# A graph attention layer on one core: 250 blocks, and destination terms with the one-hots as moving side

## The chip, the cores and the metric

The kernel runs on one core of one Trainium2 chip. It is written against the engines directly: TensorE (PE, with its weight loads as PEld), VectorE (DVE), ScalarE (ACT), GpSimd (POOL) and SyncE (SP, which issues most transfers). Each engine runs its instructions in the order in which the program gives them, and engines wait for one another by semaphores. The metric is the device time of one execution, in microseconds; lower is better.

## The reference

The input is a graph of 30000 nodes with 256 features and 510000 directed edges, sorted by destination, each of one of 8 types. One layer is computed: attention over incoming edges, then a feed-forward part with experts.

```python
feat_all = jnp.einsum('ni,rhid->rnhd', inputs, conv_weights)   # 8 types, 4 heads of 64
feat_src_e = feat_all[edge_type, edge_src]
feat_dst_e = feat_all[edge_type, edge_dst]
el = jnp.sum(feat_src_e * attn_l[edge_type], axis=-1)
er = jnp.sum(feat_dst_e * attn_r[edge_type], axis=-1)
e = jax.nn.leaky_relu(el + er, negative_slope=0.2)
m = jax.ops.segment_max(e, edge_dst, num_segments=N_NODES)
ex = jnp.exp(e - m[edge_dst])
alpha = ex / segment_sum(ex, edge_dst)[edge_dst]
h = segment_sum(alpha[..., None] * feat_src_e, edge_dst)       # + h_bias
...
x = x + gnn(layernorm(x))
x = x + ffn(layernorm(x))      # a shared MLP, and the best 2 of 4 small experts by a softmax gate
```

The score of an edge has a source term `el` and a destination term `er`, one number for each head. The change is about how `er` gets from the nodes to the edges.

## The kernel before

**Node stage.** Tiles of 128 nodes are normalised, transposed on TensorE (two transposes a tile) and multiplied by the weights of all types and heads (L304). For each node and type, a row of `feat` in DRAM gets 4 heads of 64 features with `el` as a 65th column. `er` of each node goes to `erp_d`, as three bf16 pieces whose sum is the f32 value: 4 heads x 3 pieces x 8 types = 96 columns. Between the matrix products a generator, `aside`, is asked for one small step once a tile (twice a tile after the edge records are done). Its steps prepare the edges: `edge_records` writes a record of each edge and finds the bounds of the blocks; `places` makes, for batches of 12 blocks, the lists `rk_d` (per place: index of the source row, destination, marks, penalties, and `th`, which is 1 at the edge's type and 0 at the 7 others) and `dk_d` (the destinations as 16-bit integers). `first_rows` gathers the first row of each block.

**Blocks.** The edges are cut into blocks that begin at the first destination at or after a multiple of S = 2016, with room for CAP = 2048 edges and 128 destinations. That is 252 blocks and one last block of another form. A block's edges are laid out as 128 partitions x 16 places. If a block has too many edges or nodes, or the edges are not sorted, a flag (`bad`) makes a general second pass run after this one.

**Edge loop.** It is unrolled over the blocks `t`, and each turn has six parts, c = 0 to 5, in which pieces of several blocks are put one after another by hand. The rest of the program is this order: there is no other planner. In a turn,

- `load(t+2)` asks SyncE for the block's lists, its `dr` (the destinations, copied to all partitions), `erp` (the 96 columns of the block's up to 128 nodes) and the residual; `gather(t+1)` has GpSimd fetch 15 rows of `feat` per partition (L962), SyncE the first one from `stage`;
- `dest_select` (L1009, VectorE) compares `dr` with the node numbers: a one-hot of node by edge, 128 x 2064 in bf16, in c = 4 for block t+2;
- `dest_expand` (L1026, TensorE) multiplies each of 16 columns of places (one-hot as the stationary side, 128 x 128) with `erp` (96 moving columns), four in each of four pieces; `dest_pick` (L1037, L1039, VectorE) multiplies a piece by `th` and sums over types and pieces of bf16, which gives `er` of the edges. The first piece of block t+2 is done in c = 4 and 5, the others of block t+1 in c = 0 to 3;
- `scores` (L1066 on, in c = 1) adds `er` and `el` and starts the running maxima along the destinations; `turn_ends` (TensorE, L993 and L994, c = 2), `across` (VectorE, L1084, c = 3) and `turn_back` (TensorE, L1091 and L1092, c = 4) carry them over the partitions; `softmax` (L1098 on) and `exps` come in c = 5;
- `onehot` (ScalarE, L1049 and L1050) builds the one-hot of edge by node in f32; `weigh` (VectorE, L1115) multiplies the gathered rows by the weights; `sums` (TensorE, L1122) multiplies the two, for block t-1, one sixth in each part; `finish` (L1144 to L1147) divides;
- one step of `Experts` (the feed-forward part for a group of four finished blocks: L754 to L877) is taken in each part. Its four results go out by SyncE (`put`).

An f32 matmul shows as two records on TensorE. The buffers that matter are: `dr`, `erp` and `ohT` two each, `pe` (the result of the expansion in PSUM) two, the gathered rows four blocks in a ring.

Of the kernel before, what the change touches and what calls it, by code (L numbers as in the profile page):

```python
# [10 lines left out]
F32 = mybir.dt.float32  # L11
BF16 = mybir.dt.bfloat16
# [23 lines left out]

U = 16
CAP = U * P
S = 2016
# [9 lines left out]
WR = WT + U * R // 2  # L49
# [7 lines left out]
def kernel(  # L57
# [40 lines left out]
    erp_d = dram.tile([N + P, H, 3, R], BF16, name="erp_d")  # L98
# [4 lines left out]
    rk_d = dram.tile([NBLK, P, WR], I32, name="rk_d")  # L103
    dk_d = dram.tile([NBLK * CAP + 16], I16, name="dk_d")
    stage = dram.tile([NBLK * P, H * HW], F32, name="stage")
# [3 lines left out]
    lo_d = dram.tile([KT, P], F32, name="lo_d")  # L109
    n_d = dram.tile([KT, P], F32, name="n_d")  # L110
    uns_d = dram.tile([EP], F32, name="uns_d")
    mnmx = dram.tile([2, NGRP], F32, name="mnmx")
# [21 lines left out]
    def layernorm(pool, xg, n, name, m=P):  # L134
# [10 lines left out]
        for t in range(n):  # L145
# [28 lines left out]
                   allow_small_or_imprecise_dtypes=True)  # L174
    icol = wf.tile([P, P], F32, name="icol")
# [45 lines left out]
    with ExitStack() as cx:  # L221
# [102 lines left out]
        def dest_pieces(q, n):  # L324

            er = quad.pop((q, "er"))
            del quad[q]
            erp = xp.tile([P, T, H, 3, R], BF16, name="erp")
            erv = er.rearrange("p j (r h) -> p j h r", h=H)[:, :n]
            for k in range(3):  # L330
                nc.vector.tensor_copy(erp[:, :n, :, k, :], erv)
                if k < 2:
                    nc.vector.tensor_sub(erv, erv, erp[:, :n, :, k, :])
            per_rows(q, lambda r, n: erp_d[r:r + n].rearrange("n h k r -> n (h k r)"),
                     lambda p, j: erp.rearrange("p j h k r -> p j (h k r)")[p, j], True)
# [9 lines left out]
        def edge_records(cl):  # L345
# [55 lines left out]
            nc.sync.dma_start(erp_d[N:N + P].rearrange("n h k r -> n (h k r)"),  # L401
                              zx.bitcast(BF16)[:, :R * 3 * H])
            yield

# [3 lines left out]
            dw = gp.tile([P, KT, WN + 1], I32, name="dw")  # L408
            nc.gpsimd.memset(dw, -1)
            jj = gp.tile([P, WN], F32, name="jj")  # L410
            nc.gpsimd.iota(jj, pattern=[[1, WN]], base=0, channel_multiplier=0,
                           allow_small_or_imprecise_dtypes=True)
            first = gp.tile([P, KT], F32, name="first")
            irow = gp.tile([P, 1], F32, name="irow")
# [6 lines left out]
            nc.sync.dma_start(dw[0:1, 0, 1:], dst[0:WN].rearrange("(o c) -> o c", o=1))  # L421
            for k in range(KT):
                a = 1 if k == 0 else 0
                n = min(P, NBLK + 1 - k * P)
                nc.sync.dma_start(dw[a:n, k, :],
                                  bass.AP(tensor=dst.tensor, offset=dst.offset + (k * P + a) * S - 1,
                                          ap=[[S, n - a], [1, WN + 1]]))
            before_last = gp.tile([1, 1], I32, name="before_last")
            nc.sync.dma_start(before_last, dst[E - UL * P - 1:E - UL * P].rearrange("(o c) -> o c", o=1))
            yield  # L430
            lof = gp.tile([P, 2, KT], F32, name="lof")
            miss = gp.tile([P, KT, WN], F32, name="miss")
            nc.vector.tensor_tensor(miss, dw[:, :, 1:], dw[:, :, :WN], op=ALU.is_equal)
            yield
            for i, v in enumerate((jj[:, None, :].to_broadcast([P, KT, WN]), dw[:, :, 1:])):
                cand = gp.tile([P, KT, WN], F32, name="cand")
                nc.vector.scalar_tensor_tensor(cand, miss, FAR, v, op0=ALU.mult, op1=ALU.add)
                nc.vector.tensor_reduce(lof[:, i, :], cand, AX.X, ALU.min)
                yield
            nc.vector.tensor_add(lof[:, 0, :], lof[:, 0, :], first)  # L440
            nc.vector.tensor_scalar_min(lof[:, 0, :], lof[:, 0, :], float(E))
            nc.vector.tensor_scalar(lof[:, 1, :], lof[:, 1, :], 0.0, float(N), op0=ALU.max, op1=ALU.min)
            yield
            lor = gp.tile([1, KT * P], F32, name="lor")
            nr = gp.tile([1, KT * P], F32, name="nr")
            with nc.allow_non_contiguous_dma(reason="first edges and nodes of blocks, once"):
                for i, (t_d, row) in enumerate(((lo_d, lor), (n_d, nr))):
                    nc.sync.dma_start(t_d.rearrange("k p -> p k"), lof[:, i, :])
                    yield
                    if i:  # L450
                        nc.sync.dma_start(t_d[0:1, 0:1], zx[0:1, 0:1])
                        yield
                    nc.sync.dma_start(row, t_d.rearrange("(o k) p -> o (k p)", o=1))
                    yield
# [7 lines left out]
            unm = gp.tile([EP, 1], F32, name="unm")  # L462
# [5 lines left out]
            unr = gp.tile([1, EP], F32, name="unr")  # L468
# [3 lines left out]
            two = gp.tile([1, 5], F32, name="two")  # L472
            gap = gp.tile([1, NBLK], F32, name="gap")
# [9 lines left out]
            nc.vector.tensor_reduce(bad, two, AX.X, ALU.max)  # L483

# [5 lines left out]
        def places(cl):  # L490
# [35 lines left out]
            for k, (b0, n) in enumerate(batches):  # L526
# [40 lines left out]
                d16 = kp.tile([P, GB, U], I16, name="d16k")[:, :n]  # L567
                nc.gpsimd.tensor_copy(d16, rc[:, :, :U, 1])
# [13 lines left out]
                th = o[:, :, WT:].bitcast(BF16).rearrange("p b (u r) -> p b u r", r=R)  # L582
                for b in range(0, n, GB // 2):
                    m = min(n - b, GB // 2)
                    nc.vector.tensor_tensor(th[:, b:b + m], rc[:, b:b + m, :U, 2:3].to_broadcast([P, m, U, R]),
                                            it8[:, None, :U].to_broadcast([P, m, U, R]), op=ALU.is_equal)
                    yield

                def done(o=o, d16=d16, b0=b0, n=n):
                    nc.sync.dma_start(rk_d[b0:b0 + n].rearrange("b p w -> p b w"), o)  # L590
                    nc.sync.dma_start(dk_d[b0 * CAP:(b0 + n) * CAP].rearrange("(b p u) -> p b u", p=P, u=U), d16)
# [290 lines left out]
    with ExitStack() as cx:  # L882
# [4 lines left out]
        pe_p = cx.enter_context(tc.tile_pool(name="pe", bufs=2, space=PSUM))  # L887
# [34 lines left out]
        def load(t):  # L922
# [3 lines left out]
            if s.own:  # L926
# [12 lines left out]
                s.a12 = rf[:, W1:W1 + 2 * (U + 2)].rearrange("p (i w) -> p i w", i=2)[:, :, :U]  # L939
                s.th = rk[:, WT:].bitcast(BF16).rearrange("p (u r) -> p u r", r=R)  # L940
# [11 lines left out]
            s.erp = lp.tile([P, H, 3, R], BF16, name="erp")  # L952
# [52 lines left out]
        def dest_select(t):  # L1005
# [4 lines left out]
                                    rowid[:, t:t + 1], None, op0=ALU.is_equal)  # L1010
            s.ov = ohT[:, :n * P].rearrange("n (p u) -> n u p", u=n)
            if not s.own:
                s.th = wk.tile([P, UL, R], BF16, name="th", bufs=1)
# [6 lines left out]
        def dest_expand(t, c):  # L1020

            s = blk[t]
            u0, u1 = s.dc[c], s.dc[c + 1]
            pe = pe_p.tile([P, 5, H * 3, R], F32, name="pe")
            for u in range(u0, u1):
                nc.tensor.matmul(pe[:, u - u0].rearrange("p f r -> p (f r)"), s.ov[:, u, :],  # L1026
                                 s.erp.rearrange("n h k r -> n (h k r)"), start=True, stop=True)
            s.pe = pe

        def dest_pick(t, c):  # L1030

            s = blk[t]
            if c == 0:
# [420 lines left out]
```

## Time and profile before

The median of 11 runs is 8525.87 us (8505.01 to 8543.13). The profiled execution took 8503.86 us.

| | |
|---|---|
| span of the profiled execution | 8502.1 us, 97367 instructions |
| its own time | 8503.86 us |
| PE busy | 6501.1 us, 76% |
| PEld busy | 4163.5 us, 49% |
| DVE busy | 5293.6 us, 62% |
| ACT busy | 3414.1 us, 40% |
| POOL busy | 4085.6 us, 48% |
| mean granted TensorE clock | 0.875 |
| mean DMA rate | 143 GB/s |

Busy time is the time in which an engine runs instructions; several run at once. The node stage fills some 1700 us, the edge loop the rest. Line numbers (L1026) are those of the kernel before. In a group's row stand the line, engine, operation, what is written and read with shapes, the count, then busy us and mean ns of one, and after the bar the idle time of the engine just before these, with what ended it. "Remote" stands for a semaphore whose update the profile puts down to no instruction.

### The profile page before, as it was taken

How to read it: one execution, taken by the hardware profiler on the slowest of the kernel's cores; microseconds unless marked ns; L12 is line 12 of the kernel's file. 1: busy time of each engine (PE TensorE's matmuls, PEld its weight loads, DVE VectorE, ACT ScalarE, POOL GpSimd, SP SyncE). 2: the span in 40 equal slices, each digit the busy share in tenths (PEclk: the TensorE clock that was granted, in tenths of full speed). 3: DMA queues.
4: the chain of work that ended last, by engine and by line, in shares of the span. 5: the costliest groups of instructions: out<-in, count | busy, mean ns of one | idle time of the engine just before them, and what ended most of it. 6: DMA issues, size and time to landing. Idle time of an engine off the chain costs nothing. (4 is left out here: it accounts for less than half of the span.)

```text
span 8502.1 us, 97367 instructions
## 1 busy us (share of the span) xinstructions
PE 6501.1 (76%) x25770; PEld 4163.5 (49%) x25771; DVE 5293.6 (62%) x13699; ACT 3414.1 (40%) x8758; POOL 4085.6 (48%) x4424
## 2 busy tenths in 40 slices
PE   9999999937776777777777777777767777776767
PEld 5555555525444444444444444444444444444444
DVE  5557774446666666666666666666666666666665
ACT  2222222224444444444444444444444444444444
POOL 1111115665555555555555555555555555555552
PEclk9999999968888888888888888888888888888888
DMA  6657779954444444444344344343343434433441
GB/s 230 227 184 241 225 241 319 327 178 117 116 117 116 117 116 115 117 117 118 116 117 117 115 116 117 115 116 115 114 116 116 115 116 116 121 113 114 121 116 54
DMA packets 764587, 1214.72 MB, mean 143 GB/s; under 512 B 242499, under 2 KB 602918, under 8 KB 733814
## 3 DMA queue, kind: packets, MB, share of 16 engines
q1 hardware_dynamic: 568581, 668.72, 24.0%
q0 software_dynamic: 194400, 539.40, 22.7%
q8 instruction: 209, 3.42, 0.2%
q14 instruction: 357, 2.92, 0.1%
q10 hardware_dynamic: 1040, 0.26, 0.0%
HBM read 821.54 MB, written 386.43 MB: 142 GB/s over the span
## 5 line engine op out<-in xcount | busy, mean ns | idle before, releaser
L962 POOL DMA_INDIRECT ft<-feat,rk x3798 | 3607.0, 950 | 3035.3 <-PE po L1122 1428.9
L1122 PE MATMUL po<-ft,oh 128*128 128x260 f32 x8100 | 2401.9, 437 | 387.6 <-DVE ho L1147 114.2
L1122 PEld LDWEIGHTS po<-ft,oh 128*128 128x128 f32 x8100 | 1639.9, 216 | 746.9 <-issue 413.6
L304 PE MATMUL ps<-w,xT 128*128 128x448 f32 (+1 forms) x4700 | 1707.4, 518 | 1.8 <-DMA w<-_L_gnn_conv_weights_dram 1.8
L1049 ACT ACTIVATE oh<-icol,rk 128x128 f32<-128x128 f32 x4032 | 1327.7, 389 | 57.1 <-remote 32.1
L1115 DVE TENSOR_TENSOR ft<-ft,p 128x768 f32<-128x768 f32 x1518 | 1292.3, 852 | 69.3 <-ACT ft L1108 49.2
L304 PEld LDWEIGHTS ps<-w,xT 128*128 128x128 f32 x4700 | 875.3, 190 | 688.7 <-issue 602.5
L1026 PE MATMUL pe<-erp,ohT 128*128 128x96 bf16 x4050 | 451.0, 239 | 594.4 <-DVE ohT L1009 320.8
L1037 DVE TENSOR_TENSOR ere<-pe,rk 128x384 f32<-128x384 f32 x1008 | 553.5, 549 | 506.6 <-remote 385.1
L1026 PEld LDWEIGHTS <-ohT 128*128 128x128 bf16 x4050 | 377.8, 158 | 983.8 <-issue 592.2
L306 ACT COPY fo<-ps 128x448 f32<-128x448 f32 (+1 forms) x711 | 377.9, 533 | 1060.0 <-PE ps L304 863.6
L1050 ACT ACTIVATE oh<-oh 128x384 f32<-128x384 f32 x1518 | 740.3, 488 | 55.7 <-remote 5.7
L1039 DVE TENSOR_REDUCE e<-ere 128x16 f32<-128x384 f32 (+1 forms) x1012 | 561.4, 555 | 34.7
L1107 ACT ACTIVATE p<-e 128x64 f32<-128x64 f32 (+1 forms) x253 | 70.1, 277 | 1233.4 <-DVE e L1061 1042.5
L818 PE MATMUL ph<-xT,v 128*128 128x512 f32 (+2 forms) x1024 | 495.1, 607 | 0.9 <-ACT a L819 0.5
L764 ACT COPY xT<-ph 128x512 f32<-128x512 f32 (+1 forms) x128 | 73.6, 575 | 1025.5 <-remote 871.3
L1084 DVE TENSOR_TENSOR_SCAN car<-through,t 8x128 f32<-8x128 f32 x252 | 101.5, 403 | 603.7 <-remote 485.7
L1091 PE MATMUL t<-ident,car 8*128 8x4 f32 x506 | 105.9, 277 | 429.7 <-issue 369.0
L871 PE MATMUL pf<-w,h 128*128 128x256 f32 x506 | 205.7, 495 | 269.4 <-ACT wT L864 213.4
L306 DVE COPY fo<-ps 128x448 f32<-128x448 f32 (+1 forms) x464 | 242.4, 528 | 202.2 <-PE ps L304 170.6
L818 PE MATMUL ph<-xT,w 128*128 128x512 f32 (+1 forms) x512 | 307.5, 731 | 60.8 <-ACT xT L764 34.4
L1091 PEld LDWEIGHTS t<-ident,car 8*128 8x128 f32 x506 | 83.6, 206 | 521.0 <-issue 443.7
(219 smaller groups left out, 7362.7 us busy)
## 6 DMA issues: line engine op xcount, KB each, us to landing
feat<-fo SPq DMA_DIRECT2D x234, 1040.0 KB
dr<-dk_d SPq DMA_DIRECT2D x252, 516.0 KB
ft<-feat,rk POOLq DMA_INDIRECT x3798
stage<-fr SPq DMA_DIRECT2D x84, 390.0 KB
ft<-stage SPq DMA_DIRECT2D x252, 130.0 KB
xt<-xb_d SPq DMA_DIRECT2D x253, 128.0 KB
out_dram<-og SPq DMA_DIRECT2D x253, 128.0 KB
xb_d<-xb SPq DMA_DIRECT2D x58, 512.0 KB
```

Source lines behind the costliest of these rows:

```text
L304: nc.tensor.matmul(ps, t["xT"][:, k, :], w[:, k, c0:c1], start=k == 0, stop=k == 1)
L306: eng(t["fo"][:, h0:h1, :HD], ps[:, :n].rearrange("p (a d) -> p a d", d=HD))
L818: nc.tensor.matmul(ps[:, :self.w], lhs, rhs, start=i == 0, stop=i == len(pairs) - 1)
L871: nc.tensor.matmul(pf[:M], self.h2[:, tok], w3, start=True, stop=False)
L962: nc.gpsimd.indirect_dma_start(out=s.ft[:, u].rearrange("p h d -> p (h d)"), out_offset=None, in_=feat[:, :], in_offset=bass.IndirectOffse ...
L1026: nc.tensor.matmul(pe[:, u - u0].rearrange("p f r -> p (f r)"), s.ov[:, u, :], s.erp.rearrange("n h k r -> n (h k r)"), start=True, stop=True)
L1037: nc.vector.tensor_mul(ere, s.pe[:, :u1 - u0], s.th[:, u0:u1, None, :].to_broadcast([P, u1 - u0, H * 3, R]))
L1039: nc.vector.tensor_reduce(s.e[:, :, u0:u1].rearrange("p h u -> p u h"), ere.rearrange("p u (h k) r -> p u h (k r)", h=H), AX.X, ALU.add)
L1049: nc.scalar.activation(s.oh[:, u, :], icol, AF.Abs, bias=s.nd[:, u:u + 1])
L1050: nc.scalar.activation(s.oh[:, u0:u1], s.oh[:, u0:u1], AF.Relu, bias=1.0, scale=-1.0)
L1115: nc.vector.tensor_mul(fc, fc, pc[:, :, None].to_broadcast([P, (u1 - u0) * H, HD]))
L1122: nc.tensor.matmul(s.po.rearrange("n h d -> n (h d)"), s.oh[:, u, :], s.ft[:, u].rearrange("p h d -> p (h d)"), start=u == 0, stop=u == s. ...
```

## The change

The constant S becomes 2032, so that there are 250 blocks and the last one. A block may now begin at the destination boundary before or after its multiple of S; four candidate lists (edge and node, early and late) are made, and a scan picks for each block the one that keeps it within CAP edges and 128 nodes.

The destination terms change sides. The block's `erp` piece (128 nodes x 32 columns: 4 heads x 8 types) is now the stationary side, and the one-hot of node by edge is the moving side, 512 columns at a time. The four quarters of the block's 2048 places go to the four 32-partition parts of one PSUM bank, and the three bf16 pieces add up there: 12 matmuls, all in c = 0. In `rel_d` each place has its type; it is loaded to the 32 partitions of each quarter by four transfers a block. One VectorE operation (c = 2) compares it with the partition's type and multiplies by the PSUM result. Four f32 matmuls with a 128 x 16 selector (`dest_turn`, c = 3) turn the result back to edges by heads, where `scores` reads it from PSUM. `dest_select` moves from c = 4 to c = 5, behind the softmax. `pe` gets one buffer, `ee` the other.

In the node stage, `places` no longer makes `th`; the lists get shorter by 64 words of 178. The place numbers and types are transposed on TensorE (four transposes a batch) and copied by ScalarE to 16-bit rows, which are stored in four transfers a batch instead of one. The last block keeps the old form.

```diff
-S = 2016
+S = 2032
...
-WR = WT + U * R // 2
+WR = WT
...
+    sel = wf.tile([P, 4 * H], F32, name="sel")
...
+    rid = wf.tile([P, 1], F32, name="rid")
...
+            nc.vector.tensor_tensor_scan(late[:, 1:NBLK + 1], may[:, 1], may[:, 0], 1.0, ALU.add, ALU.max)
...
-                th = o[:, :, WT:].bitcast(BF16).rearrange("p b (u r) -> p b u r", r=R)
-                for b in range(0, n, GB // 2):
-                    m = min(n - b, GB // 2)
-                    nc.vector.tensor_tensor(th[:, b:b + m], rc[:, b:b + m, :U, 2:3].to_broadcast([P, m, U, R]),
-                                            it8[:, None, :U].to_broadcast([P, m, U, R]), op=ALU.is_equal)
-                    yield
-
-                def done(o=o, d16=d16, b0=b0, n=n):
+                yield
+                GH2 = GB // 2
+                ps = pf.tile([P, 512], F32, name="ps").rearrange("q (i f p) -> q i f p", i=2, p=P)
+                rt = kp.tile([GH2 * U, 2, 2, P], I16, name="rt")
+                parts = [(f, b, min(n - b, GH2)) for f, b in enumerate(range(0, n, GH2))]
+                for i in range(2):
+                    for f, b, m in parts:
+                        nc.tensor.transpose(ps[:m * U, i, f], dr2[:, i, b:b + m].rearrange("p b u -> p (b u)"), ident)
+                for f, b, m in parts:
+                    nc.scalar.copy(rt[:m * U, :, f], ps[:m * U, :, f])
+                yield
+
+                def done(o=o, rt=rt, parts=parts, b0=b0, n=n):
                     nc.sync.dma_start(rk_d[b0:b0 + n].rearrange("b p w -> p b w"), o)
-                    nc.sync.dma_start(dk_d[b0 * CAP:(b0 + n) * CAP].rearrange("(b p u) -> p b u", p=P, u=U), d16)
+                    for i, d in enumerate((dk_d, rel_d)):
+                        for f, b, m in parts:
+                            nc.sync.dma_start(d[(b0 + b) * CAP:(b0 + b + m) * CAP].rearrange("(q p) -> q p", p=P),
+                                              rt[:m * U, i, f])
...
-        pe_p = cx.enter_context(tc.tile_pool(name="pe", bufs=2, space=PSUM))
+        pe_p = cx.enter_context(tc.tile_pool(name="pe", bufs=1, space=PSUM))
+        ee_p = cx.enter_context(tc.tile_pool(name="ee", bufs=1, space=PSUM))
...
+                s.rel = lp.tile([P, 4 * P], I16, name="rel")
+                for c in range(4):
+                    e0 = t * CAP + c * 4 * P
+                    nc.sync.dma_start(s.rel[32 * c:32 * c + 32], rel_d[e0:e0 + 4 * P].partition_broadcast(32))
...
         def dest_expand(t, c):
 
-            s = blk[t]
+
+            s = blk[t]
+            if s.own:
+                if c == 0:
+                    s.pe = pe_p.tile([P, 4 * P], F32, name="pe", tag="pe")
+                    for k in range(3):
+                        for q in range(4):
+                            nc.tensor.matmul(s.pe[32 * q:32 * q + 32], s.erp[:, k].rearrange("n h r -> n (h r)"),
+                                             s.ohT[:, q * 4 * P:(q + 1) * 4 * P], start=k == 0, stop=k == 2)
+                return
...
         def dest_pick(t, c):
 
             s = blk[t]
+            if s.own:
+                if c == 0:
+                    s.pick = wk.tile([P, 4 * P], F32, name="pick")
+                    nc.vector.scalar_tensor_tensor(s.pick, s.rel, rid, s.pe, op0=ALU.is_equal, op1=ALU.mult)
+                return
...
+        def dest_turn(t):
+
+            s = blk[t]
+            if not s.own:
+                return
+            s.ee = ee_p.tile([P, 4, 4 * H], F32, name="ee")
+            for j in range(4):
+                nc.tensor.matmul(s.ee[:, j], s.pick[:, j * P:(j + 1) * P], sel, start=True, stop=True)
...
-            nc.vector.tensor_add(s.e, s.e, s.ft[:, :, :, HD].rearrange("p u h -> p h u"))
+            if s.own:
+                s.e = wk.tile([P, H * UL], F32, name="e", bufs=3)[:, :H * U].rearrange("p (h u) -> p h u", h=H)
+                nc.vector.tensor_add(s.e.rearrange("p h (c j) -> p h c j", c=4),
+                                     s.ee.rearrange("p j (c h) -> p h c j", c=4),
+                                     s.ft[:, :, :, HD].rearrange("p (c j) h -> p h c j", c=4))
...
-                        at(dest_pick, t + 2, 0)
-                    if c == 4:
                         at(dest_select, t + 2)
...
-                    if 0 < c < 4:
-                        at(dest_pick, t + 1, c)
+                    if 0 < c < 5 and t + 1 == NBLK:
+                        at(dest_pick, t + 1, c - 1)
...
+                    if c == 2 and t + 1 < NBLK:
+                        at(dest_pick, t + 1, 0)
...
-                    if c == 4:
-                        at(dest_expand, t + 2, 0)
-                    if c < 3:
-                        at(dest_expand, t + 1, c + 1)
+                    if c < 4:
+                        at(dest_expand, t + 1, c)
+                    if c == 3:
+                        at(dest_turn, t + 1)
```

## The prediction

> **What bounds the kernel now.** I began with the busy time by stretch, because a mean over the span mixes two programs. Columns: start:end, length, then busy us (and instructions) of PE, PEld, DVE, ACT and POOL, granted clock, DMA share, GB/s.
>
> ```profile
> 0.00:1600.00 1600.00, 1593.49 (x4794) 865.74 (x4796) 956.44 (x2621) 415.81 (x889) 387.48 (x535) 1.00 0.73 244
> 1900.00:8420.00 6520.00, 4669.83 (x20128) 3151.93 (x20128) 4184.23 (x10664) 2899.48 (x7622) 3506.46 (x3692) 0.85 0.40 116
> 5176.00:5200.00 24.00, 6.86 (x29) 5.09 (x29) 6.66 (x15) 7.69 (x20) 15.25 (x17) 0.70 0.43 124
> 5200.00:5283.00 83.00, 70.50 (x306) 47.84 (x305) 61.92 (x161) 42.32 (x113) 44.05 (x47) 0.90 0.40 115
> ```
>
> The node stage (first row) is all TensorE. In the edge loop (second row) no engine is full: TensorE 72%, VectorE 64%, DMA 40%. The last two rows cut one group of four blocks in two: 24 us in which every engine that computes is mostly idle, and 83 us in which TensorE is 85% busy and VectorE 75%. So most blocks are nearly TensorE-bound, and one place in four blocks is a stall.
>
> Next, the groups of the loop (2200 to 8300 us) for what the change touches.
>
> ```profile
> L962 POOL DMA_INDIRECT ft<-feat,rk x3471 | 3296.6, 950 | 2804.4 <-PE po L1122 1342.1 <-issue 737.6 <-remote 309.7
> L1039 DVE TENSOR_REDUCE e<-ere 128x16 f32<-128x384 f32 x927 | 514.1, 555 | 31.8
> L1037 DVE TENSOR_TENSOR ere<-pe,rk 128x384 f32<-128x384 f32 x927 | 508.9, 549 | 428.9 <-remote 333.3 <-PE po L1122 54.0 <-PE ph L818 19.3
> L1026 PE MATMUL pe<-erp,ohT 128*128 128x96 bf16 x3708 | 412.8, 238 | 513.6 <-DVE ohT L1009 302.1 <-issue 148.8 <-remote 62.7
> L1009 DVE TENSOR_SCALAR ohT<-dr,rowid 128x2064 bf16<-128x2064 int16 x232 | 296.7, 1279 | 0.0
> L858 DVE TENSOR_TENSOR a<-a,ph 128x512 f32<-128x512 f32 x115 | 78.5, 682 | 192.0 <-remote 158.0 <-PE po L1122 27.1 <-PE ph L855 6.4
> ```
>
> 3471 gathers at 15 a block are 231.4 blocks in 6100 us: 26.4 us a block, 105.4 a group. By the shares above a block holds 18.9 us of TensorE and 16.9 of VectorE. GpSimd's gathers need 15 x 1.25 us = 18.8 us, so it isn't the bound.
>
> The stall, in VectorE's timeline (start, duration, what, and idle time before it):
>
> ```profile
> 5188.76 0.41 DVE L1084 TENSOR_TENSOR_SCAN car<-through,t 8x128 f32<-8x128 f32 x1 [11.51 <-remote]
> 5195.87 0.56 DVE L1037 TENSOR_TENSOR ere<-pe,rk 128x384 f32<-128x384 f32 x1 [5.59 <-remote]
> 5196.94 1.28 DVE L1009 TENSOR_SCALAR ohT<-dr,rowid 128x2064 bf16<-128x2064 int16 x1
> 5198.73 0.28 DVE L1098 TENSOR_TENSOR c<-t,rk 128x128 f32<-128x128 f32 x1
> ```
>
> The two waits are for TensorE's semaphore, which moves at 5188.74 and 5195.85, while the records of the matmuls waited for end at 5175.6 and 5175.9. I cannot say what holds these signals. Some 16 us a group go here (24 less the 8 that 6.86 us of TensorE would take at 85%).
>
> **The change, part by part.**
>
> *Two blocks fewer.* 253 blocks become 251: -2 x 26.4 = -53 us. From the reference's destinations I worked out the new bounds: no block over 2048 edges or 128 nodes, so the second pass stays off.
>
> *VectorE.* Out, per block: four products and four sums, 4 x (0.549 + 0.555) = 4.4 us. In: one operation on 128x512 from PSUM, 0.68 us by L858, the nearest row. Net -3.7 us of 16.9. The score addition reads PSUM with the same 64 columns. How much reaches the end? At least nothing, if TensorE alone sets clean blocks. At most 3.4 us, TensorE's idle 15% of a clean block of (105.4 - 16) / 4 = 22.4 us. TensorE's waits on VectorE (one-hots 302, denominators and outputs 251, scan rows 131 us in the loop) are 3.0 us a block, and VectorE's load falls by 22%: 0.7 us. Moving the one-hot build (1.28 us) from part 4, where the expansion and the sums queued behind it, to part 5 behind the softmax adds 0.2. In part 0 the sums already wait for the denominators, so the expansion moved there fills idle time. I take -0.9.
>
> *TensorE, expansion.* Before: four bf16 matmuls and the step to the next line take 0.29 us (5029.00 to 5029.29 below), 1.2 us a block.
>
> ```profile
> 5027.68 0.38 PE L994 MATMUL t<-turned,fb 128*8 128x128 f32 x2
> 5027.99 1.08 PE L843 MATMUL ph<-a,v 128*64 128x512 f32 x4
> 5029.00 0.45 PE L1026 MATMUL pe<-erp,ohT 128*128 128x96 bf16 x4
> 5029.29 0.89 PE L1122 MATMUL po<-ft,oh 128*128 128x260 f32 x3
> ```
>
> After: twelve matmuls of 32 stationary and 512 moving columns, to four quarters of the output partitions. L843 is the row that tells most: two matmuls of 64 columns to two halves start 7 ns apart, and the pair takes 1.01 us where one f32 matmul of full width takes 2 x 0.43 (L818's spacing). So parts side by side cost about what one does. A bf16 matmul of 512 columns is not in the trace: at most 0.43 us (an f32 record of that width), at least half, 0.21; L1026's 63 ns for 96 columns scale to 0.33. I take 0.27, so three rounds of 0.27 and 0.19 for changing the column mode twice (312 ns from L1122 to an 8-column matmul where 219 is its own step) are 1.0 us; bounds 0.8 to 1.5, all overlapped, and 2.7 to 5.3 if nothing overlaps. Four quarters at once have no row.
> The Trainium skill, "TensorE: Matmul & The Clock Gate", Part 3, measured three column tiles at 2.38 times the speed of one, short of three; with that page's 216 ns for one such matmul, four at the same efficiency (3.17) would make the twelve take 12 x 0.216 / 3.17 = 0.8 us, an estimate, and by it the sum would be 0.2 us a block lower, some 30 us at the end. This case's halves (1.01 us against 0.86) agree that parts side by side cost a little more than one, and no run here shows four yet.
>
> *TensorE, turning back.* Four f32 matmuls with 128x128 stationary and 16 moving columns, eight records. The gate matmuls are that shape:
>
> ```profile
> 5204.65 1.84 PE L770 MATMUL pg<-gw,xT 128*128 128x4 f32 x16
> ```
>
> Eight take 0.92 us. TensorE thus gains 1.0 + 0.92 - 1.2 = +0.75 us, and about +0.85 with the half clock that the loop's 0.85 contains. Following the waits back from 8300 to 2200 us, TensorE's own work is some 43% of that path, 61% of its busy time: +0.5 us a block reaches the end. The turn sits in part 3, ahead of the sums there, and waits for the pick of part 2: what queues behind are three sums, whose input VectorE finishes just before the pick, so 0 to 0.7 us; I take 0, as TensorE has two transposed rows, a layer and two sums to do first.
>
> *The stall.* After the late signal VectorE runs L1037, L1039, L1009 and one product before the softmax (L1098), 2.9 us in which others wait. Pick and one-hot are gone from there: up to 2.4 us a group. I take 1.5 x 62 groups = -93 us; bounds below, under the rivals.
>
> *Loads.* SyncE issues four more transfers a block (0.35 to 0.7 us each by its other issues, so about 2 us of 26) and 128 KB more, with 32 KB less of indices. Behind them in its queue are the one-hot source, factors, residual and first rows; the one-hot source of that group was issued at 5166.0 and used at 5196.9, so 30 us of slack hide it. Without that cover it would cost those 2 us a block, 500 us. New buffers wait on the pick two blocks back, earlier than the boundary scan that the same load already waits for.
>
> *Node stage.* TensorE is full there, so 84 transposes at 0.109 us and their starts land: +12 us. The expanded types (42 x 1.1 us of VectorE) go, beside other work: 0. Eleven more steps ahead of the place lists, one a tile of 7.3 us, shift these by 80 us; they end at 1260 us of 1600: 0, and their stores get fewer, longer rows.
>
> **The sum.** The profiled execution took 8503.9 us (span 8502.1): - 53 + 250 x (-0.9 + 0.5) - 93 + 12 = 8270. It lies 22 us below the median of the runs shown (8525.9), so I forecast 8290.
>
> **The rivals.**
> 1. *Quarters run one after another (slower).* Twelve at 0.27 are 3.2 us, +2.25 over my 1.0; at 61% over 250 blocks +340: 8630. It decides from about 2.5 us for the twelve. For: no row has four parts. Against: L843. 12%.
> 2. *VectorE was not on the path (slower).* TensorE's 85% in clean blocks speaks for it, its 3.0 us of waits on VectorE against. Without the -0.9 a block and the -93: 8290 + 225 + 93 = 8608. 15%.
> 3. *The second late signal goes.* The expansion's result, for which L1037 waits at 5195.87, is now made ten microseconds earlier and asked for in another part. If its 7.1 us (5188.74 to 5195.85) vanish in each group: 62 x (7.1 - 1.5) = -347: 7943. For: only this place shows it. Against: the hold may simply move to the next signal. 12%.
> 4. *The change does not do what it says:* the second pass runs, another loop of at least 6500 us: about 14,800. My bounds exclude it for this input. 1%.
>
> **How the numbers follow.** Forecast 60%. A measurement of this kernel can tell 0.2%, 17 us. Forecast (nearly all) and rival 3 are faster: 0.68; a small part of the forecast and of rival 2 lie within: 0.04; the rest slower: 0.28. The range takes 8290 down by the 3.4 us bound on VectorE's relief or half of rival 3, and up to rivals 1 and 2: 7980 to 8640. The likeliest case's own range is 8130 to 8450.
>
> **What would show it.** L1037 and L1039 at the last block alone; one product of 0.7 us a block instead; the 12 matmuls as groups of four a few ns apart, about 1.0 us in all, after it 0.9 us of turning; TensorE in the clean stretches at 88 to 92%; block time about 25.6 us (231 blocks in 5920 us); the scan's wait (L1084) still there. Wrong it would be if the twelve take over 2.5 us, if TensorE's clean share stays at 85% with longer blocks, if the pick waits for its landing places, or if the stall grows or goes.

## The result: 2.3% faster where 2.8% was forecast, and a stall that moved

| | before | after |
|---|---|---|
| median of the runs | 8519.46 us (31 runs) | 8327.81 us (8 runs, 8315.36 to 8334.11) |
| span of the profiled execution | 8502.1 us | 8336.9 us |
| TensorE busy | 6501.1 us | 6609.0 us |
| VectorE busy | 5293.6 us | 4378.7 us |
| mean granted clock | 0.875 | 0.879 |

The ratio is 0.9773, with a 95% interval of 0.976 to 0.9786. 8290 was forecast, 38 us below; the fall is 192 us where 236 was forecast. One execution among those below (the pick issued six times) took 11490.98 us at a granted clock of 0.62, and no time or ratio here counts it.

Busy time by stretch of the changed kernel, columns as in the prediction: node stage, edge loop, and one group of four blocks cut into its stall and the rest.

```profile
0.00:1600.00 1600.00, 1582.92 (x4812) 862.27 (x4814) 911.77 (x2572) 422.12 (x919) 375.35 (x543) 1.00 0.74 234
1900.00:8260.00 6360.00, 4790.08 (x21086) 3108.27 (x21087) 3350.92 (x8959) 2889.37 (x7630) 3502.86 (x3683) 0.85 0.42 122
5186.00:5210.00 24.00, 9.30 (x37) 6.66 (x37) 3.69 (x8) 4.93 (x13) 14.90 (x17) 0.64 0.39 105
5210.00:5289.00 79.00, 67.73 (x308) 42.96 (x309) 50.85 (x139) 42.09 (x113) 42.54 (x45) 0.94 0.44 129
```

In the loop TensorE went from 72 to 75%, VectorE from 64 to 53%. In the clean stretch TensorE is at 86% (85 before), VectorE at 64% (75 before). The 24 us in which little is computed are still there.

Groups of the loop (2200 to 8100 us) for what the change touched.

```profile
L1028 POOL DMA_INDIRECT ft<-feat,rk x3449 | 3280.6, 951 | 2620.4 <-issue 730.9 <-DVE e L1197 703.9 <-PE po L1218 437.2
L1096 PE MATMUL pe<-ohT,erp 128*32 128x512 bf16 x2748 | 231.5, 443 | 56.0 <-issue 47.1 <-PE po L1218 4.5 <-DVE ohT L1075 4.1
L1130 PE MATMUL ee<-sel,pick 128*128 128x16 f32 x1832 | 227.0, 256 | 0.0
L1112 DVE SCALAR_TENSOR_TENSOR pick<-rel,rid,pe 128x512 f32<-128x512 int16 x230 | 170.6, 742 | 6.7 <-PE t L1060 4.2 <-PE po L1218 2.4
L1180 DVE TENSOR_TENSOR_SCAN car<-through,t 8x128 f32<-8x128 f32 x229 | 92.5, 404 | 989.4 <-remote 895.5 <-issue 87.9 <-PE t L1060 4.8
```

3449 gathers at 15 a block are 229.9 blocks in 5900 us: 25.66 us a block, 26.4 before. One pick of 0.742 us a block has taken the place of the eight operations. L1180 is the boundary scan (L1084 before): it waits 895.5 us for a signal of TensorE. Its row before (2200 to 8300 us, 231 blocks; the changed kernel's stretch holds 230):

```profile
L1084 DVE TENSOR_TENSOR_SCAN car<-through,t 8x128 f32<-8x128 f32 x232 | 93.5, 403 | 558.2 <-remote 443.2 <-issue 87.0 <-PE po L1122 22.7
```

Before, this wait (443.2) and that of L1037 (333.3) were 776 us together. So the stall has changed its place, and by this wait it has not become smaller. VectorE's timeline shows it (start, duration, what, idle time before it):

```profile
5204.97 0.41 DVE L1180 TENSOR_TENSOR_SCAN car<-through,t 8x128 f32<-8x128 f32 x1 [17.67 <-remote]
5205.41 0.21 DVE L1181 COPY turn<-car 8x128 f32<-8x128 f32 x1
5205.55 1.53 DVE L1211 TENSOR_TENSOR ft<-ft,p 128x768 f32<-128x768 f32 x2
5209.65 0.29 DVE L1194 TENSOR_TENSOR c<-t,rk 128x128 f32<-128x128 f32 x1 [2.56 <-PE po L1218]
```

The matmul waited for (L1060) has its record end at 5185.99; its semaphore update comes at 5204.94. Outside such stretches the update follows a record's end by some 14 ns. Inside them updates come one by one, at multiples of about 0.71 us (5206.40, 5207.15, 5207.87, 5208.58, 5209.32), and then the rest in a burst some 40 ns apart. Many of SyncE's steps take 0.7 us in the same stretches (0.68 to 0.73 here). What goes on beside it is in GpSimd's timeline:

```profile
5179.21 0.95 POOL L1028 DMA_INDIRECT ft<-feat,rk  x1 [0.30 <-PE po L1218]
5180.46 0.95 POOL L1028 DMA_INDIRECT ft<-feat,rk  x1 [0.30 <-issue]
5181.72 0.95 POOL L1028 DMA_INDIRECT ft<-feat,rk  x1 [0.30 <-issue]
...
5196.74 0.94 POOL L1028 DMA_INDIRECT ft<-feat,rk  x1 [0.30 <-issue]
5197.99 0.95 POOL L1028 DMA_INDIRECT ft<-feat,rk  x1 [0.30 <-issue]
5200.25 0.94 POOL L1028 DMA_INDIRECT ft<-feat,rk  x1 [1.31 <-remote]
```

From 5177.96 to 5197.99 seventeen gathers follow one another every 1.25 us without a break. This became the theory to test, after another one (the square root) had fallen.

### The profile page after: what moved, and what is told of

The parts are those of the page before. It is cut to its first block, busy times and chain, and to the rows that moved or that the text cites. A ratio compares the mean times of both kernels' runs of the same rounds, so it can differ in the third digit from the quotient of the medians.

```text
span 8336.9 us, 98524 instructions
## 1 busy us (share of the span) xinstructions
PE 6609.0 (79%) x26710; PEld 4108.5 (49%) x26711; DVE 4378.7 (53%) x11884; ACT 3394.5 (41%) x8748; POOL 4064.8 (49%) x4418
## 5 line engine op out<-in xcount | busy, mean ns | idle before, releaser
L1218 PE MATMUL po<-ft,oh 128*128 128x260 f32 x8036 | 2323.5, 425 | 372.6 <-issue 226.9
L1218 PEld LDWEIGHTS po<-ft,oh 128*128 128x128 f32 x8036 | 1577.4, 207 | 995.4 <-issue 689.8
L1211 DVE TENSOR_TENSOR ft<-ft,p 128x768 f32<-128x768 f32 x1506 | 1272.5, 851 | 214.9 <-issue 155.4
L1180 DVE TENSOR_TENSOR_SCAN car<-through,t 8x128 f32<-8x128 f32 x250 | 100.9, 404 | 1041.6 <-remote 944.3
L1203 ACT ACTIVATE p<-e 128x64 f32<-128x64 f32 x251 | 69.5, 277 | 1239.1 <-DVE e L1151 865.4
L1194 DVE TENSOR_TENSOR c<-t,rk 128x128 f32<-128x128 f32 x250 | 72.5, 290 | 562.9 <-PE t L1188 213.2
L1096 PE MATMUL pe<-ohT,erp 128*32 128x512 bf16 x3000 | 255.3, 448 | 132.5 <-issue 53.9
L939 DVE TENSOR_TENSOR og<-pf,x 128x256 f32<-128x256 f32 x251 | 106.5, 424 | 449.1 <-PE pf L936 435.7
L1075 DVE TENSOR_SCALAR ohT<-dr,negp 128x2064 bf16<-128x2064 int16 x250 | 319.6, 1278 | 23.6 <-DMA stage<-fr 18.1
```

Of the source, the lines that this page charges most:

```text
L1075: nc.vector.tensor_scalar(ohT[:, :3 * s.dw].rearrange("n (i e) -> n i e", i=3), s.dr[:, :, :s.dw], negp if s.own else rowid[:, t:t + 1], N ...
L1096: nc.tensor.matmul(s.pe[32 * q:32 * q + 32], s.erp[:, k].rearrange("n h r -> n (h r)"), s.ohT[:, q * 4 * P:(q + 1) * 4 * P], start=k == 0, ...
L1211: nc.vector.tensor_mul(fc, fc, pc[:, :, None].to_broadcast([P, (u1 - u0) * H, HD]))
L1218: nc.tensor.matmul(s.po.rearrange("n h d -> n (h d)"), s.oh[:, u, :], s.ft[:, u].rearrange("p h d -> p (h d)"), start=u == 0, stop=u == s. ...
```

## The experiments

Ratios are to the kernel before on the same chip, with their 95% intervals; the changed kernel's is 0.9773 (0.976 to 0.9786). Where two kernels are compared in us, their ratios' difference times 8519 us is taken.

**The order of the twelve matmuls.**

```diff
-                    for k in range(3):
-                        for q in range(4):
+                    for q in range(4):
+                        for k in range(3):
```

> The changed kernel with the twelve expansion matmuls in another order: the three pieces of one quarter of the partitions follow each other, then the next quarter, so that neighbours in the queue use the same 32 columns of TensorE. Theory (the quarters run beside one another only if issued next to each other): each of the twelve takes the 0.21 us step that a round of four takes now, 2.5 us from first to last start in place of 0.45, so about +2 us of TensorE a block; at the 61% that the prediction took as reaching the end this is +300 us (8630), with all of it on the path +500. Rival (TensorE runs them side by side in any order, or their cost lies hidden): under +50 us, and starts still a few ns apart.

8330.58 us, 0.9765 (0.9741 to 0.9788): no difference. TensorE's timeline still has the twelve as one run:

```profile
3019.51 0.86 PE L1096 MATMUL pe<-ohT,erp 128*32 128x512 bf16 x12 [0.90 <-issue]
```

The twelve starts come in three rounds of four, 0.22 us apart, in both kernels; from first to last start it is 0.47 us here and 0.45 us in the changed kernel. One after another, at 0.22 us each, the twelve starts would lie 2.4 us apart from first to last. So the four quarters run beside one another also when the program names them one after another (a record does not tell its quarter; this is read from the starts).

**VectorE's relief given back.**

```diff
+                    for _ in range(6):
                         nc.vector.scalar_tensor_tensor(s.pick, s.rel, rid, s.pe, op0=ALU.is_equal, op1=ALU.mult)
```

> The changed kernel with the pick operation issued six times in place of once, same input and output: 5 x 0.742 = +3.7 us of VectorE a block, which is what the change had taken away. Theory (VectorE's relief counts in part, 0.9 us of 3.7 by the prediction): +225 us or more, about 8550; it may be more than the relief was, since the turn and the expansion's next buffer wait behind the pick: up to +930 if all of it lies on the path. Rival 2 of the prediction (VectorE was not on the path): under +60 us.

8427.5 us, 0.989 (0.9856 to 0.9924): +100 us over the changed kernel, 0.40 us a block (give or take 0.12) for 3.7 us of work. The groups (2200 to 8000 us) show that the work was done:

```profile
L1113 DVE SCALAR_TENSOR_TENSOR pick<-rel,rid,pe 128x512 f32<-128x512 int16 x1337 | 998.6, 747 | 58.9 <-remote 19.5
```

It is between the two: VectorE's time counts, but 11% of the added work reached the end, not the quarter that I had taken.

**The turn three times.**

```diff
-            for j in range(4):
+            for j in (0, 1, 2, 3) * 3:
```

> The changed kernel with the four turning matmuls issued three times, same input and output: 2 x 0.81 = +1.6 us of TensorE a block. Theory (61% of TensorE's time reaches the end): +250 us, about 8580. If TensorE now sets the clean blocks alone: +405 us. If VectorE or the gathers set them: under +60 us.

8253.01 us, 0.9674 (0.9646 to 0.9702): 84 us *faster* than the changed kernel, with 1.6 us more of TensorE a block. No theory allowed that. The waits of the loop (2200 to 8000 us; waited in all, times, longest) say where it came from:

```profile
POOL ft L1028 <- PE po L1218: 1020.5, 438, 15.9
DVE pick L1112 <- remote: 447.7, 53, 10.8
```

The stall's wait is now at the pick, 8.4 us each time where the scan waited 17, and GpSimd's gathers wait more for TensorE (1020.5 us, 427.3 in the changed kernel in the same stretch). TensorE has no fixed price here: with the longer turn the stall moved again, and that outweighed its own time. Why it moved is not shown.

**The square root off ScalarE.**

```diff
-            nc.scalar.activation(self.rs[:M, 0, :self.n], self.mv[:M, :self.n, 1], AF.Sqrt, bias=eps[:M])
+            nc.vector.tensor_scalar_add(v, self.mv[:M, :self.n, 1], EPS)
+            nc.vector.tensor_scalar(y.bitcast(I32), v.bitcast(I32), -0.5, 1597463007.0, op0=ALU.mult, op1=ALU.add)
+            for i in range(3):
...
-                nc.vector.reciprocal(rs[:, 0, :n], rs[:, 0, :n])
```

> The changed kernel with the square root of the feed-forward part's normalisation taken from ScalarE and worked out on VectorE (a first guess from the number's bits and three Newton steps, eleven operations on 120x4 a group, some 1 us). ScalarE then never loads another function table in the edge loop; now it does so twice a group, 1.28 us each. In the trace of the changed kernel the stretches in which TensorE's semaphore updates come late begin at or within 2 us of the table load for the square root. Theory S (that load, or the drain around it, starts the stall): the wait of the boundary scan falls from 17 us to under 5 and the time by 62 x 10 or more, to 7500 to 7750. Rival (the loads that come in a bunch behind the output stores start it, and the table load only falls into the same place): the scan's wait stays at 15 us or more and the time changes by no more than the two table loads, 0 to -160 us.

8367.91 us, 0.9815 (0.9789 to 0.9841): slower by 36 us, just clear of the changed kernel's interval. No table load is left in the loop's trace, and the scan (L1186 here) waits as before:

```profile
DVE car L1186 <- remote: 864.1, 55, 17.6
```

Theory S falls. The table load only stands in the same place.

**Pauses between the gathers.**

```diff
+        idle = cp.tile([P, 1024], F32, name="idle")
...
+                if u % 3 == 0:
+                    nc.gpsimd.memset(idle, 0.0)
```

> The changed kernel with one idle operation on GpSimd (it fills a scratch tile of 128x1024 with zeros, some 0.95 us) behind every third gather, five a block, so that no more than three gathers follow one another directly. In the traces so far the slow steps of 0.71 us on SyncE are 7 to 8% of its steps when fewer than three gathers have just followed one another every 1.25 us, 41% behind six to eight and over 70% behind nine or more, and TensorE's semaphore comes in the same steps. Theory G (long unbroken runs of gathers hold back the semaphores): the 17 us wait of the boundary scan falls under 5, the time to 7700 to 8000. Rival (the bunch of loads behind the output stores holds them, and the runs of gathers only follow from the late lists): the stall stays, GpSimd is busy 23.8 of 25.7 us a block, and the time is 8330 to 8480.

7651.14 us, 0.8963 (0.8941 to 0.8985): 8% less than the changed kernel. Theory G's forecast holds, even a little beyond its 7700, by an edit that only adds work to GpSimd. The gathers and the pauses in its timeline:

```profile
5200.18 0.95 POOL L1029 DMA_INDIRECT ft<-feat,rk  x1 [0.17 <-issue]
5201.44 0.95 POOL L1029 DMA_INDIRECT ft<-feat,rk  x1 [0.30 <-issue]
5202.69 0.97 POOL L1029 DMA_INDIRECT ft<-feat,rk  x1 [0.30 <-issue]
5203.65 0.96 POOL L1033 MEMSET idle<- 128x1024 f32 x1
5204.78 0.95 POOL L1029 DMA_INDIRECT ft<-feat,rk  x1 [0.17 <-issue]
```

The scan's wait for a remote signal is gone from the waits. SyncE's steps of 0.66 to 0.76 us fall from 961 of 6918 to 286 of 7221 (2200 to 8000 us). In the group's row GpSimd has no idle time left but its own steps, so it is now the bound: 4.59 us for three gathers and a pause, 22.9 us a block. The transfers were not what was too slow before: by the packets' records a gather has landed 2.47 us after its start in the median in the changed kernel, 2.48 us here. Nor is the rival's bunch of loads enough by itself: SyncE still waits for the output stores, with the next loads behind them (807.6 us in 2200 to 7500 us here, 562.5 us in 2200 to 8000 us of the changed kernel), and the stall is gone.

**The stores later.**

```diff
-                groups[q] = Experts(xc, ph_p, pc_p, x1, n, lambda i, r, q=q: put(q + i, r))
+                groups[q] = Experts(xc, ph_p, pc_p, x1, n, lambda i, r, q=q: puts.append([6, lambda: put(q + i, r)]))
...
+                    for p in puts:
+                        p[0] -= 1
+                    while puts and puts[0][0] <= 0:
+                        puts.pop(0)[1]()
...
```

> The changed kernel with each output store put into SyncE's queue six parts (one block) later than its result is made, so that SyncE doesn't wait for it (now 563 us in the loop) with the next loads behind it. Theory G: with the lists on time, the gathers don't start ten microseconds late once a group and then run 12 to 22 in a row; the stall shrinks and the time falls by 200 to 600 us. The rival with the bunch of loads says the same of this run; the two differ on the run before. If neither the bunch nor the runs matter: within 30 us of 8328.

7829.17 us, 0.9173 (0.915 to 0.9196): -511 us against the changed kernel. With the lists on time the gathers no longer stop for ten microseconds in each group and then catch up; they wait for TensorE a little at a time instead (2200 to 7500 us). The longest unbroken run falls from 22 to 16 (2200 to 8000 us).

```profile
POOL ft L1028 <- PE po L1218: 875.3, 544, 6.6
DVE car L1180 <- remote: 1.5, 1, 1.5
```

The slow steps on SyncE are still 12% (14 in the changed kernel), and VectorE's other operations still wait for remote signals (DVE g L846 227.7 us, DVE den L1242 213.1 us). Runs of twelve gathers and more have hardly become fewer, 49 after 58. So this run fits theory G only in part: what it took away are the longest runs and the scan's wait, not the long runs as such.

**The number of blocks alone.**

```diff
-S = 2032
+S = 2016
```

> The changed kernel with S = 2016, so 252 blocks and the last one, as before. The prediction's step (two blocks at the price of a block): 2 x 25.66 = +51 us, 8379. Rival (the time hangs on the 510,000 edges, not on the blocks, since GpSimd and the sums are not what is full): under +15 us.

8385.38 us, 0.9826 (0.9801 to 0.985): 45 us more by the ratios, 58 by the medians, around the 51 of the step.

**The one-hot build back in part 4.**

```diff
                         at(softmax, t)
                         at(exps, t)
+                    if c == 4:
                         at(dest_select, t + 2)
```

> The changed kernel with the one-hot build of node by edge (L1075, 1.28 us) back in part 4, ahead of the weighing there. The prediction's step (moving it to part 5, behind the softmax, brought 0.2 us a block): +50 us, 8380. Rival (the place doesn't matter, as the matmuls that use it come only in the next turn): within 20 us.

8341.79 us, 0.9766 (0.9741 to 0.9791): no difference. The rival holds.

**The same pauses, all behind the fifteenth gather.**

```diff
+        idle = cp.tile([P, 1024], F32, name="idle")
...
+                if u == s.u - 1:
+                    for _ in range(5):
+                        nc.gpsimd.memset(idle, 0.0)
```

> The changed kernel with the same five idle operations on GpSimd a block as in the run with pauses behind every third gather (128x1024, 0.95 us each), but all five behind the fifteenth gather. GpSimd's time a block is the same, and the gathers of a block may again follow one another directly. Theory G (what counts is how many gathers run without a break): most of that gain goes; 8100 to 8350, slow steps on SyncE back above 10%. Rival (the gain came from GpSimd's slower mean pace, which leaves the next block's rows to a later time): 7650, as with the pauses spread.

8788.41 us, 1.0322 (1.0305 to 1.0339): the whole gain goes, and 468 us more. The scan's wait is back (2200 to 7500 us):

```profile
DVE car L1184 <- remote: 566.5, 47, 12.8
```

The work on GpSimd is the same, and only where the pauses stand differs. So the mean pace alone does not decide, and theory G's direction holds: slow steps on SyncE are 678 of 6468 (2200 to 8000 us), above 10% as forecast. Its size does not: 8100 to 8350 was forecast, and what the loss beyond the changed kernel comes from is not shown.

**Shorter pauses.** The edit is shown against the run with a pause behind every third gather.

```diff
-        idle = cp.tile([P, 1024], F32, name="idle")
+        idle = cp.tile([P, 448], F32, name="idle")
```

> The changed kernel with pauses behind every third gather as before, but of 128x448 in place of 128x1024: some 0.45 us in place of 0.95. In the run with 0.95 us, VectorE's scores waited 767 us for gathers in 5300 us of the loop, GpSimd was busy 83% and a block took 22.75 us. Theory G with GpSimd as the next bound: a short pause breaks the runs as well and leaves GpSimd 2.5 us a block, so 7300 to 7600. Rival (the pause has to be long enough for something to drain): the stall comes back in part, 7700 to 8200.

8391.61 us, 0.9847 (0.9815 to 0.9878): my forecast missed, the rival is nearer, and even it expected less than a full return. No run is longer than three gathers now, yet the stall is back, so run length alone does not decide either: the pause has to be long enough (2200 to 7500 us).

```profile
L1033 POOL MEMSET idle<- 128x448 f32 x1019 | 498.6, 489 | 0.3
DVE c L1197 <- remote: 779.6, 49, 19.2
```

The stall stands at the softmax now, 49 times up to 19.2 us.

**The kernel before, with the long pauses.** The edit is that of the pauses above, on the kernel before.

> The kernel before, with the pauses of 0.95 us behind every third gather that took the changed kernel to 7651. It tells what the change is worth where the stall is gone. Theory 1 (GpSimd then sets the pace: three gathers and a pause take 4.59 us, 22.9 us a block, and the changed kernel's block took 22.75): only the two blocks are left, 7651 + 2 x 22.8 = 7697, within 40 us. Theory 2 (the engines' work counts also there, by the 0.5 to 0.6 us a block that the change brought beyond the two blocks): some 7830. Theory 3 (VectorE's 16.9 us and its order set the clean blocks of the kernel before): above 7900.

7657.86 us, 0.8969 (0.8954 to 0.8984), against 0.8963 for the changed kernel with them: here the change is worth nothing that can be measured. The two groups' rows (2200 to 7500 us), first the kernel before, then the changed one:

```profile
L963 POOL DMA_INDIRECT ft<-feat,rk x3464 | 3291.9, 950 | 893.6 <-issue 600.0 <-PE po L1125 132.8 <-PE pe L1029 33.3
```

```profile
L1029 POOL DMA_INDIRECT ft<-feat,rk x3466 | 3291.7, 950 | 894.0 <-issue 651.2 <-PE po L1221 110.4 <-DVE e L1161 26.2
```

3464 and 3466 gathers in 5300 us: both go at GpSimd's pace, 22.95 us a block, behind which any time that the change saves on other engines would be hidden. Theory 1 holds, but for the 46 us of the two blocks, of which 15 are left in the spans: the changed kernel's first gather starts 27 us later (1781.4 against 1754.0).

**Three long pauses a block.**

```diff
-                if u % 3 == 0:
+                if u in (4, 8, 12):
```

> The changed kernel with the long pause (128x1024, 0.95 us) but only three a block, behind the fourth, eighth and twelfth gather. So far 1.53 us a gather on the mean (three and a long pause) was free of the stall, 1.37 (three and a short pause) and 1.25 (none) were not. Here the mean is 1.46 with runs of four. Theory L (a run may be four long if the pause is long enough): GpSimd has 21.9 us or less a block, and the time is 7350 to 7650. Theory M (GpSimd's share of time in gathers must stay near 62%; here it is 65%, with short pauses it was 70%): part of the stall is back, 7700 to 8100.

8322.27 us, 0.9745 (0.9726 to 0.9764): as slow as the changed kernel. Both theories gave less. VectorE's waits for remote signals are fewer than in the changed kernel, but TensorE itself waits (2200 to 7500 us):

```profile
PEld ph L880 <- issue: 573.2, 736, 11.9
DVE c L1197 <- remote: 296.5, 43, 12.5
```

The step lies between this pattern (1.46 us a gather in four and a pause) and that of three and a pause (1.53). The run is not as clean as it was meant to be: no pause follows a block's last three gathers, and in 58 places they run on into the next block's four, seven in a row. So it does not tell whether the four or the sevens bring the stall back.

## Why the prediction was right, point by point

The time fell, and by an amount near the forecast, but the terms were not the ones I had set, and two errors cancelled. In the two profiled executions, first gather to last went from 6629.9 to 6429.7 us (-200.2): two blocks at 26.34 are -52.7, and -147.5 are left, 0.59 us for each of 250 blocks. I had 0.4 a block and 93 us of stall, 0.77 together. The first gather starts 26 us later, the tail after the last is 9 us longer, and the sum is the -165.2 of the spans. (The medians are 192 us apart: the profiled execution of the changed kernel took 8338.66 us, more than any of the eight runs.)

Of the 147.5 us, 100 are VectorE's by the price that putting its work back showed, and the stall gave between nothing and 61 by the time in which the three engines are all idle (below). What is left for TensorE is then between 48 us gained and 14 us lost. That is an estimate from these figures and not a measurement; I had 125 us lost. So VectorE's worth was set 125 us too high and TensorE's cost 111 us or more too high, and that these two cancel is luck.

- *Two blocks:* right; -53 forecast, 45 to 58 measured by itself.
- *VectorE:* the work was sized rightly, the pick at 0.742 us for 0.68, the net at -3.4 us a block (16.9 to 13.5) for -3.7. Its worth was not: 3.7 us put back cost 0.40 us a block, where I had -0.9 for the change. With TensorE's price this is the term that was most mis-sized. The 0.2 of it for the later one-hot build is nothing (8341.79 us with the build back in part 4).
- *TensorE:* the expansion is dearer by my sum (1.0 us) than on the chip: 0.45 us from first to last start and 0.22 for the last round; to the next line it is 0.76 at least where the trace grants the full clock, 1.40 where it grants half. The turn took 0.81 us for 0.92. TensorE's busy time rose by 0.4 us a block (18.9 to 19.3), not 0.75, and its share of the clean stretch to 86%, not the 88 to 92 forecast. The 61% as its price didn't hold: 1.6 us more came out 84 us faster.
  The Trainium skill, "TensorE: Matmul & The Clock Gate", Part 3, has three column tiles at 2.38 times one; the estimate from it was 0.8 us for the twelve. The trace is nearer to that than to my 1.0: twelve steps of 0.22 us would be 2.6 us, and they took 0.67, 3.9 times less. No run here shows three.
- *The stall:* the weakest step. I gave back 1.5 us of it in each group because fewer operations stand between the late signal and the softmax. Whether it shrank depends on the measure. VectorE's wait rose from 776 to 895.5 us. The time in which TensorE, VectorE and ScalarE are all idle fell from 875 us (2200 to 8300 us before) to 814 us (2200 to 8100 us), in as many blocks, so by this 61 us went where I had 93. Followed back through the waits as the prediction did (8300 to 2200 us before, 8100 to 2200 us after), late signals with no known sender fell from 4.9 to 3.4 us a block and VectorE's work from 6.4 to 3.3, while TensorE's rose from 11.8 to 14.7: TensorE took most of the place that the others left on this path. By my own sign (wrong if the stall grows) the wait speaks against the step. What the pauses show is that the rhythm of GpSimd's gathers sets the stall, which the prediction left open.
- *Node stage:* +12 forecast, +26 measured at the first gather of the profiled execution.
- *Loads:* the 30 us of slack hid them: no transfer stands among the waits of the pick's row (6.7 us of idle time in all). SyncE is held for 1855 us of the loop by the wait for the scan's result anyway, ahead of the new transfers.
- *The range:* its lower end does not follow from the bounds named. The 3.4 us bound on VectorE's relief is 625 us below the forecast, half of rival 3 is 174, and 7980 is 310.

Of the rivals, the first (quarters one after another) is excluded by the starts: the twelve take 0.67 us, in the other order 0.69, where it needed 2.5. The second (VectorE not on the path) is excluded by the 100 us that VectorE's work cost when it was put back, though at 0.40 us a block that is nearer to nothing than to my 0.9. In the third, the second late signal did go, but not its 7.1 us a group: "the hold may simply move to the next signal" is what happened, in one wait of 17 us.

What stays open is how a stretch of closely spaced gathers holds back the semaphores of TensorE and the steps of SyncE. The runs show that pauses between the gathers, in both kernels, take the stall away, that shorter pauses or the same ones in one place do not, and that the transfers themselves aren't late. They don't show what the three engines share, nor whether it is the length of a run or the pace within it that counts; the run with later stores lost the scan's wait and kept runs of fifteen.

## What to carry to other kernels

When an engine waits for a semaphore whose matmul has long ended in the trace, look for what runs unbroken beside it, on an engine that isn't full, before the waiting engines are relieved. Here the whole change was worth 2.3%, some 1.2% of it by work taken off VectorE, and pauses on GpSimd, an engine with time to spare, 8% more (7651 us, the fastest of all the kernels here). With them GpSimd sets the pace, and the change no longer shows. Price an engine's time by adding work to it, and expect the sign to surprise you while a stall of this kind stands.

## What was not expected of the hardware

- Gathers on GpSimd every 1.25 us for a dozen and more in a row went with TensorE's semaphore updates coming up to 19 us late, in steps of 0.71 us. At 1.53 us a gather (three, then 0.97 us of another operation) the big stalls were gone; at 1.46 (four, with some runs of seven) and at 1.37 (three, then 0.49 us) they were not, nor with the five pauses of a block all in one place. Each gather took 0.95 us and landed after some 2.5 us all the while.
- Where the pauses stand counts more than how many there are: five behind each block's last gather cost 468 us over none, the same five behind every third saved 690.
- Four matmuls of 32 columns, to four quarters of the partitions, start 3 to 4 ns apart and share one 0.22 us step; when the program has three for one quarter before the next, they start 10 to 23 ns apart and share it still.
